# Second feed-forward product of eight layer 0 blocks in a seven-product form, and two bias additions on GpSimd

## The chip, the core and the metric

The kernel runs on one core of one Trainium2 chip, as one launch. The core has five engines that take their own instruction streams in order and signal each other by semaphores: TensorE (PE) multiplies matrices and writes to PSUM, VectorE (DVE) and ScalarE (ACT) work on tiles element by element and can read PSUM, GpSimd (POOL) does the indirect DMAs and small work, and SyncE (SP) issues most plain DMAs. The metric is the device time of the launch in microseconds (us); less is better.

## The reference

Two graph transformer layers over 2708 nodes with 512 features. What is computed in each layer, for node features h and an adjacency matrix adj:

```python
mask = adj + eye(n)
q, k, v = h @ Wq.T + bq, h @ Wk.T + bk, h @ Wv.T + bv        # 8 heads of 64
scores = einsum('nhd,mhd->hnm', q, k) / sqrt(64), -1e9 where mask == 0
ctx = softmax(scores) @ v
h1 = layer_norm(h + ctx @ Wo.T + bo, ln1_g, ln1_b)
ff = relu(h1 @ W1.T + b1) @ W2.T + b2                        # 512 -> 2048 -> 512
h2 = layer_norm(h1 + ff, ln2_g, ln2_b)
```

Everything is float32. The adjacency matrix is sparse: few nodes have more than a dozen neighbours, so the kernel attends over lists of neighbours and not over a full score matrix.

## The kernel before

The work is done by `by_edges`. The 2708 nodes are cut into 22 tiles of 128 (the last has 20), ordered by how many neighbours their nodes have, and pairs of tiles make 11 blocks. First the neighbour lists are made and layer 0's keys, values and queries are projected; then each layer runs over its 11 blocks, k = 0 to 10. Block 10 holds the short tile.

For one block, `feed_forward` is a generator with 16 steps, f = 0 to 15, one for each 128 of the 2048 hidden features. In step f, TensorE computes the hidden chunk `pf` (four products of 128x128 by 128x256, L1503, both tiles of 128 nodes at once), ScalarE writes relu of it to the tile `ft` (L1514), and TensorE does the second product of the chunk three steps back (`second(f - LAG)`, L1476): for each of the block's two tiles, 128x128 of `ft` by 128x512 of W2, added up in the PSUM tiles `a0` and `a1`. At the end the accumulators are added to the residual rows (L1547) and normed (`norm`, L1257 to L1267; its power on GpSimd, L1263).

Between the steps the main loop, written out by hand, puts other work into the same instruction streams; each engine keeps that order (the schedule is manual). In step 5 to 8 comes `keys_values` of the block before: its rows z are transposed, and the next layer's k and v are projected (L606); the key bias is added by VectorE on the way out of PSUM (L1578). In steps 10 to 12 comes `attended` for the next block: the context tile is transposed, projected to `o`, the gathered input rows are added (L1435), then the output bias in layer 0 (L1438), and the sum is normed. In step 15 `turned` transposes the normed rows into `hT` for the next block.

The attention itself is a generator too (`attend`). It is cut into chunks of up to two neighbours for each node of a tile; for a chunk, GpSimd gathers key and value rows (L1099), VectorE multiplies keys by queries (L1136) and reduces (L1142), ScalarE exponentiates (L1155) and scales values (L1162), VectorE scales the first value row (L1168) and adds up (L1175). `advance` moves it on by so many chunks in each step, from the tables PACES and PACE. Gathered rows lie in a ring of five tiles and, in layer 0 after the first queries, a sixth in the place of the query weights ("wq").

PSUM has eight banks of 512 float32 columns: two for `a0` and `a1`, three in the ring "f" for the hidden chunks, three in the ring "g" for transposes and projections.

## Time and profile before

| | us |
|---|---|
| median of three runs | 1844.04 (1843.19 to 1844.4) |
| the profiled execution, its own time | 1843.06 |
| the profiled execution, its span | 1841.3 |
| PE busy in the span | 1827.6 (99%) |
| DVE busy | 1374.8 (75%) |
| ACT busy | 947.2 (51%) |
| POOL busy | 785.4 (43%) |

The span is the stretch of the profiled execution from its first to its last instruction; its own time is a little longer, and the runs' median stands beside both. An engine's busy time is the union of its instructions. A timeline row gives start, length, engine, line, operation, tiles and how many such instructions follow each other. A window row gives, for a stretch, the busy time of PE, of its weight loads, of DVE, ACT and POOL (with counts), then the granted clock, the DMA share and GB/s. A wait row gives who waited for whom, the sum in us, how many times, and the longest. A group row ends in busy us and mean ns of one, and in the idle time before them. Layer 0's blocks run from about 250 us to 1080 us.

### The profile page before, as it was taken

To read this page: it belongs to the slowest core of one execution; us is meant where nothing else is said; L and a number is where in the kernel's file an instruction comes from. 1 tells how busy PE (TensorE), PEld (TensorE's weight loads), DVE (VectorE), ACT (ScalarE), POOL (GpSimd) and SP (SyncE) were. 2 spreads that over 40 slices of the span, in tenths; PEclk is the share of its full clock that TensorE was granted. 3 is DMA by queue.
4 is the path that set the end of the run, shared out by engine and by line. 5 is a ranking of instruction groups with operands and counts; after the bars stand their busy time and mean duration, and the time that the engine had idled before them with its cause. 6 is when DMAs were issued, how large, how long until landed. Compare 5 with 4: busy or idle time off the path is not lost.

```text
span 1841.3 us, 20983 instructions
## 1 busy us (share of the span) xinstructions
PE 1827.6 (99%) x6195; PEld 1092.1 (59%) x6195; DVE 1374.8 (75%) x2147; ACT 947.2 (51%) x3263; POOL 785.4 (43%) x745
## 2 busy tenths in 40 slices
PE   9999999999999999999999999999999999999998
PEld 4444456565666656566565544666666666666666
DVE  4996778776877767777774147977888898889853
ACT  4770445554546455555643204665655675566531
POOL 3334755543535444444431032444554554456302
PEclk9999999999999999999999999999999999999999
DMA  9997987644646455463631676835554564555300
GB/s 332 374 336 265 372 277 245 214 156 163 209 151 222 139 205 183 148 206 108 224 121 46 214 249 265 315 129 200 186 199 168 211 246 150 210 195 184 137 18 21
DMA packets 129829, 368.01 MB, mean 200 GB/s; under 512 B 14378, under 2 KB 32670, under 8 KB 129704
## 3 DMA queue, kind: packets, MB, share of 16 engines
q0 software_dynamic: 70608, 252.12, 39.3%
q1 hardware_dynamic: 48938, 92.85, 14.2%
q10 hardware_dynamic: 10158, 21.61, 3.1%
q8 instruction: 50, 0.82, 0.2%
q14 instruction: 75, 0.61, 0.1%
HBM read 315.84 MB, written 50.68 MB: 199 GB/s over the span
## 4 chain that ended last, share of the span: by engine, by line
PE 96%; DVE 2%; ACT 1%; issue 1%; DMA 0%; POOL 0%; POOLq 0%; DVEq 0%
PE pf L1503 31%; PE a L1476 30%; PE k L606 8%; PE q L606 8%; PE v L606 8%; PE o L606 8%; PE tp L1273 3%; PE a L1491 0%; DMA zT<-zT_d 0%; PE pf L1476 0%; DVE sc L1142 0%; DVE kv L1136 0%; ACT kv L1162 0%; POOL rd L1263 0%; ACT hT L1278 0%
## 5 line engine op out<-in xcount | busy, mean ns | idle before, releaser
L1503 PE MATMUL pf<-hT,w 128*128 128x256 f32 (+1 forms) x2816 | 631.4, 371 | 0.1
L1503 PEld LDWEIGHTS pf<-hT,w 128*128 128x128 f32 x2816 | 516.1, 190 | 163.0 <-issue 100.3
L1099 POOL DMA_INDIRECT kv<-kv_d,listed x420 | 506.2, 1205 | 247.7 <-issue 118.4
L1476 PE MATMUL a<-w,ft 128*128 128x512 f32 x1312 | 611.1, 592 | 0.0
L1476 PEld LDWEIGHTS a<-w,ft 128*128 128x128 f32 x1312 | 246.8, 190 | 187.4 <-issue 167.5
L1514 ACT ACTIVATE ft<-pf,b 128x256 f32<-128x256 f32 (+1 forms) x336 | 154.1, 461 | 336.3 <-PE pf L1503 328.7
L1263 POOL TENSOR_TENSOR rd<-va,mhalf 128x1 f32<-128x1 f32 (+1 forms) x88 | 81.3, 924 | 565.4 <-DVE va L1261 564.9
L1162 ACT ACTIVATE kv<-kv,p 128x64 f32<-128x64 f32 x1232 | 311.0, 335 | 5.0
L1136 DVE TENSOR_TENSOR kv<-kv,q 128x1024 f32<-128x1024 f32 (+1 forms) x222 | 257.0, 1158 | 15.9 <-DMA q<-q_d,ident_i 13.6
L1142 DVE TENSOR_REDUCE sc<-kv 128x16 f32<-128x1024 f32 (+1 forms) x222 | 258.0, 1162 | 7.6
L1175 DVE TENSOR_TENSOR acc<-acc,kv 128x1024 f32<-128x1024 f32 (+2 forms) x178 | 205.3, 1153 | 50.9 <-ACT kv L1162 34.1
L1155 ACT ACTIVATE p<-sc,listed 128x8 f32<-128x8 f32 x420 | 104.4, 299 | 144.1 <-DVE sc L1142 97.7
L606 PE MATMUL o<-wo,cT 128*128 128x512 f32 x336 | 150.9, 593 | 1.1 <-ACT cT L1278 1.1
L1168 DVE TENSOR_TENSOR kv<-kv,p 128x512 f32<-128x512 f32 (+1 forms) x178 | 122.8, 690 | 25.7 <-ACT p L1155 22.6
L1435 DVE TENSOR_TENSOR h<-o,xb 128x512 f32<-128x512 f32 (+1 forms) x44 | 30.4, 690 | 109.5 <-PE o L606 93.3
L606 PEld LDWEIGHTS o<-wo,cT 128*128 128x128 f32 x336 | 63.5, 190 | 81.0 <-issue 73.4
L731 DVE MAX8 tops<-code 128x8 f32<-128x247 f32 (+2 forms) x242 | 78.9, 400 | 27.5 <-ACT code L726 27.5
L1267 DVE SCALAR_TENSOR_TENSOR h<-h,rd,ln_b 128x512 f32<-128x512 f32 (+1 forms) x88 | 66.1, 751 | 41.1 <-POOL rd L1263 41.1
L1206 ACT ACTIVATE cx<-acc,su 128x64 f32<-128x64 f32 (+1 forms) x352 | 88.3, 333 | 12.8 <-DVE su L1198 6.2
L1162 ACT ACTIVATE acc<-kv,p 128x64 f32<-128x64 f32 (+1 forms) x352 | 88.8, 334 | 1.4
L726 ACT ACTIVATE code<-aj 128x1354 bf16<-128x1354 int32 (+1 forms) x44 | 73.6, 1724 | 25.5 <-POOL aj L720 20.6
L1278 ACT ACTIVATE cT<-tp,bv 128x128 f32<-128x128 f32 (+1 forms) x176 | 49.0, 360 | 72.9 <-PE tp L1273 72.9
(186 smaller groups left out, 1569.9 us busy)
## 6 DMA issues: line engine op xcount, KB each, us to landing
aj<-in_adj SPq DMA_DIRECT2D x42, 677.0 KB
kv_d<-kvs ACTq DMA_DIRECT2D x21, 512.0 KB
xg<-in_xT SPq DMA_DIRECT2D x19, 512.0 KB
w<-in_W SPq DMA_DIRECT2D x16, 512.0 KB
kv<-kv_d,listed POOLq DMA_INDIRECT x420
zT_d<-zT SPq DMA_DIRECT2D x22, 256.0 KB
xb_d<-h SPq DMA_DIRECT2D x21, 256.0 KB
q<-q_d SPq DMA_DIRECT2D x21, 256.0 KB
```

What stands on the lines that cost most here:

```text
L606: nc.tensor.matmul(o[:r], xs(c), wm[:, c, :], start=(c == 0), stop=(c == NC - 1))
L1099: return nc.gpsimd.indirect_dma_start(out=to, out_offset=None, in_=table[:, :], in_offset=bass.IndirectOffsetOnAxis(ap=s, axis=0), bounds_ ...
L1136: nc.vector.tensor_tensor(kv[:r, :c, :DM], kv[:r, :c, :DM], self.q[:r].unsqueeze(1).to_broadcast([r, c, DM]), ALU.mult,)
L1142: nc.vector.tensor_reduce(self.sc[:r, s0 : s0 + c, :], kv[:r, :c, :DM].rearrange("p s (h d) -> p s h d", d=DK), AX.X, ALU.add,)
L1155: nc.scalar.activation(p[:r, s, :], self.sc[:r, s, :], AF.Exp, bias=minus[:r, g, s : s + 1])
L1162: nc.scalar.activation(to[:, i, hd], kv[:r, i, DM + h * DK : DM + (h + 1) * DK], AF.Copy, scale=p[:r, s0 + i, h : h + 1],)
L1168: nc.vector.tensor_tensor(to[:, 0, :].rearrange("p (h d) -> p h d", d=DK), kv[:r, 0, DM:].rearrange("p (h d) -> p h d", d=DK), p[:r, s0, : ...
L1175: nc.vector.tensor_tensor(self.acc[:r, :c, :], self.acc[:r, :c, :], kv[:r, :c, DM:], ALU.add)
L1206: nc.scalar.activation(cx[:r, hd], self.acc[:r, 0, hd], AF.Copy, scale=self.su[:r, h : h + 1])
L1476: nc.tensor.matmul(a[:r, cols], fts[f][:, c0 : c0 + r], self.w2[f // 2][:, f % 2, cols], start=(f == 0), stop=(f == NFC - 1),)
L1503: nc.tensor.matmul(pf[:, :w], self.w1[f // 2][:, c, f % 2 * P : f % 2 * P + P], hT[:, c, :w], start=(c == 0), stop=(c == NC - 1),)
L1514: nc.scalar.activation(ft[:, :w], pf[:, :w], AF.Relu, bias=self.b1[:, f : f + 1])
```

## The change

The second product of eight blocks of layer 0 (k = 2 to 9) takes another form. Two hidden chunks f0, f1 and the two tiles of nodes make a 2x2 matrix of 128x128 blocks; the four quarters of the W2 rows of that pair make another. For the first seven of the eight chunk pairs a Strassen-Winograd form computes their product with seven block products of 256 columns (`feed_forward_by_seven`, `products`), after four VectorE additions of 128x128 (`sums`) on the hidden chunks. The products of pair j are issued two pairs behind the hidden chunks, the sums one pair behind. The results add up in four PSUM tiles, a0, a1, c0 and c1, and eight VectorE additions and one ScalarE copy put them together at the end of the block. The eighth pair is multiplied as before.

The combinations of W2's quarters that the form needs are made in block 1 by VectorE (`form`, at the steps in FORMS): one stays in place of a quarter of W2, three go to DRAM (`form_d`), and are read back pair by pair through three single tiles (`slots`) in the former place of the query weights; the sums and two more `ft` tiles lie there as well. SyncE issues those reads as each product frees its slot. In block 9 the replaced quarter is read again from W2 (`form_back`).

PSUM rings "f" and "g" have two banks instead of three in those blocks. The gathered rows of layer 0 no longer use the query weights' place. The pace of the attention in those blocks is PACE7. Two bias additions go to GpSimd: the output bias is added to the gathered input rows ahead of time (`settled_rows`, blocks 1 to 10), and the key bias of the next layer is added to the copied key rows (ScalarE copies k from PSUM) except in the last block.

```diff
+PACE7 = (0.0,) * 3 + (0.75,) * 2 + (1.2,) * 4 + (0.75,) * 2 + (0.0,) * 2 + (0.85,) * 3
+FORMED = 1
+FORMS = (3, 5, 7, 9, 13, 14, 15)
...
+    def places_of_psum(n, more=False):
+        nonlocal ps_f, ps, ps_s
+        stage.close()
+        ps_f = stage.enter_context(tc.tile_pool(name="ps_f", bufs=n, space=PSUM))
+        ps = stage.enter_context(tc.tile_pool(name="ps", bufs=n, space=PSUM))
+        if more:
+            ps_s = stage.enter_context(tc.tile_pool(name="ps_s", bufs=1, space=PSUM))
...
-        elif n < NL - 1 and all_made and not places:
-            places.extend([None] * KVB + ["wq"])
...
+        def settled_rows(self, block, xbs):
+            for g, xb in zip(block, xbs):
+                r = size(g)
+                nc.gpsimd.tensor_tensor(xb[:r], xb[:r], self.bo[:r], ALU.add)
+            self.with_bo = True
...
-                if self.n == 0:
+                if not with_bo:
                     nc.vector.tensor_tensor(h[:r], h[:r], self.bo[:r], ALU.add)
...
+        def form(self, j):
+            w, W = self.w2[j], 2 * P
+            b11, b12, b21, b22 = w[:, 0, :W], w[:, 0, W:], w[:, 1, :W], w[:, 1, W:]
+            t2, t3, t4 = self.slots
+            nc.vector.tensor_tensor(t3, b22, b12, ALU.subtract)
+            nc.vector.tensor_tensor(b12, b12, b11, ALU.subtract)
+            nc.vector.tensor_tensor(t2, b22, b12, ALU.subtract)
+            nc.vector.tensor_tensor(t4, b21, t2, ALU.subtract)
+            for i, t in enumerate((t2, t3, t4)):
+                nc.sync.dma_start(out=form_d[j, i], in_=t)
...
+            def sums(j):
+                f0, f1 = fts[2 * j], fts[2 * j + 1]
+                s = self.sums[j % 2]
+                nc.vector.tensor_tensor(s[:, 0], f1[:, P:], f0[:, P:], ALU.add)
+                nc.vector.tensor_tensor(f0[:, P:], f0[:, :P], f0[:, P:], ALU.subtract)
+                nc.vector.tensor_tensor(s[:, 1], s[:, 0], f0[:, :P], ALU.subtract)
+                nc.vector.tensor_tensor(s[:, 2], f1[:, :P], s[:, 1], ALU.subtract)
+            def products(j):
+                f0, f1, w, s = fts[2 * j], fts[2 * j + 1], self.w2[j], self.sums[j % 2]
+                t2, t3, t4 = self.slots
+                first, last = j == 0, j == J - 1
+                for to, left, right, start, stop in (
+                    (a1[:, L], f1[:, P:], t4, first, False),
+                    (c0[:, R], s[:, 1], t2, first, False),
+                    (c1[:, L], f0[:, P:], t3, first, False),
+                    (c0[:, L], f0[:, :P], w[:, 0, L], False, last),
+                    (a0[:, L], f1[:, :P], w[:, 1, L], first, False),
+                    (c1[:, R], s[:, 0], w[:, 0, R], False, last),
+                    (a0[:, R], s[:, 2], w[:, 1, R], False, False),
+                ):
+                    nc.tensor.matmul(to, left, right, start=start, stop=stop)
+                self.ask_forms(base + min(3 * j + 6, 3 * J + 3 * (k < NB - 2)))
+                if k == NB - 2:
+                    self.form_back(j)
...
+                if f % 6 < 4:
+                    ft = dn.tile([P, W], F32, tag="ft", name="ft", bufs=4)
+                else:
+                    ft = self.more_fts[f % 2]
+                nc.scalar.activation(ft, pf[:, :W], AF.Relu, bias=self.b1[:, f : f + 1])
+                fts.append(ft)
+                if f % 2 == 0 and j > 0:
+                    sums(j - 1)
+                if f % 2 and j > 1:
+                    products(j - 2)
+                yield None
+            products(J - 1)
...
+            nc.scalar.copy(u2, c0[:, L])
+            nc.vector.tensor_tensor(zA[:, L], u2, zA[:, L], ALU.add)
+            nc.vector.tensor_tensor(u2, c0[:, R], u2, ALU.add)
+            nc.vector.tensor_tensor(pair(u34), pair(c1), twice(u2), ALU.add)
+            nc.vector.tensor_tensor(zB[:, R], c1[:, R], zB[:, R], ALU.add)
+            nc.vector.tensor_tensor(zA, a0, zA, ALU.add)
+            nc.vector.tensor_tensor(zB, a1, zB, ALU.add)
+            nc.vector.tensor_tensor(zA[:, R], u34[:, R], zA[:, R], ALU.add)
+            nc.vector.tensor_tensor(pair(zB), pair(zB), twice(u34[:, L]), ALU.add)
...
-                nc.vector.tensor_tensor(kv[:r, :DM], k[:r], self.bk[:r], ALU.add)
-                plus_rest(kv[:r, :DM], k, r)
+                if block == blocks[-1]:
+                    nc.vector.tensor_tensor(kv[:r, :DM], k[:r], self.bk[:r], ALU.add)
+                    plus_rest(kv[:r, :DM], k, r)
+                else:
+                    nc.scalar.copy(kv[:, :DM], k)
...
+                if block != blocks[-1]:
+                    nc.gpsimd.tensor_tensor(kv[:, :DM], kv[:, :DM], self.bk, ALU.add)
...
+            seven = n == 0 and FORMED < k < NB - 1
+            if n == 0 and k == FORMED:
+                now.prepared()
+            if n == 0 and k in (FORMED + 1, NB - 1):
+                places_of_psum(3 - seven, seven)
...
+                if xbs and f == 9 + 2 * (k == 0):
+                    now.settled_rows(blocks[k + 1], xbs)
-                advance((PACE if k else PACES)[n][f])
+                advance((PACE7 if seven else (PACE if k else PACES)[n])[f])
...
+                if n == 0 and k == FORMED and f in FORMS:
+                    now.form(FORMS.index(f))
```

## The prediction

> **What bounds the kernel now.** First the page: busy times, the slices and the chain that ended last.
>
> ```profile
> PE 1827.6 (99%) x6195; PEld 1092.1 (59%) x6195; DVE 1374.8 (75%) x2147; ACT 947.2 (51%) x3263; POOL 785.4 (43%) x745
> PEclk9999999999999999999999999999999999999999
> PE 96%; DVE 2%; ACT 1%; issue 1%; DMA 0%; POOL 0%; POOLq 0%; DVEq 0%
> PE pf L1503 31%; PE a L1476 30%; PE k L606 8%; PE q L606 8%; PE v L606 8%; PE o L606 8%; PE tp L1273 3%; PE a L1491 0%; DMA zT<-zT_d 0%; PE pf L1476 0%; DVE sc L1142 0%; DVE kv L1136 0%; ACT kv L1162 0%; POOL rd L1263 0%; ACT hT L1278 0%
> ```
>
> TensorE is the bound, at full granted clock, and the second product (L1476) is 30% of the chain. Busy is not proof of packed, so next the timeline where a layer 0 block starts.
>
> ```profile
> 627.45 1.02 PE L1476 MATMUL a<-w,ft 128*128 128x512 f32 x2
> 628.30 7.07 PE L1503 MATMUL pf<-hT,w 128*128 128x256 f32 x32
> ...
> 656.73 1.88 PE L1476 MATMUL a<-w,ft 128*128 128x512 f32 x4
> ```
>
> 32 records in 7.07 us with the last one showing about 0.38: one record each 0.216 us. Four of 512 columns in 1.88 with a last of 0.59: 0.43 each (0.429 from start to start). L1503 has 2816 records for 22 blocks x 16 x 4 = 1408 products, so a product is two records: 0.432 us at 256 columns, 0.858 at 512. Nothing lies between them. Last, what VectorE (DVE) has left, in the window answer and in its waits of 393 to 942 us (seven blocks).
>
> ```profile
> 427.00:505.00 78.00, 78.00 (x265) 47.94 (x264) 62.18 (x85) 42.78 (x160) 36.06 (x31) 1.00 0.51 171
> 505.00:583.00 78.00, 78.00 (x264) 47.85 (x263) 58.03 (x78) 40.40 (x150) 36.82 (x33) 1.00 0.54 186
> ```
>
> ```profile
> DVE h L1435 <- PE o L606: 31.8, 11, 4.3
> DVE kvs L1578 <- PE k L606: 31.2, 13, 4.6
> DVE acc L1175 <- ACT kv L1162: 22.5, 21, 1.6
> DVE kv L1168 <- ACT p L1155: 18.1, 14, 2.0
> DVE h L1267 <- POOL rd L1263: 12.6, 28, 0.5
> ```
>
> A block lasts 78.3 us: PE all of it, DVE about 58 (third figure with a count). Its 20 idle us are 9 waiting for PE, which go when PE hurries, and 8.5 for ACT and POOL, which need not.
>
> **What the change removes.** In k=2 to 9, seven of eight chunk pairs take 7 products of 256 columns for 4 of 512: 7x0.432 = 3.02 for 3.43 us, 0.41 less. 8x7 = 56 pairs: **22.8 us**. The eighth pair costs the same (2x0.858 + 4x0.432). Each product has its own weights: PEld 190 ns fits under 216, as in L1503. A block becomes 75.5 us if PE never waits, so stalls of 2.85 us a block give everything back.
>
> **What it adds.** DVE has no 128x128 row; 128x48 takes 208 ns and 128x264 takes 421, so 128x128 is estimated at 0.29, 128x256 at 0.41. 28 operations for the sums: 8.1 us. Block end: four adds of 256 and four of 512 (0.69) for two: +3.1. L1438 and L1578 leave (2x0.69 each): -2.8. DVE goes from 58 to 66.6 of 75.5; with the 8.5 of waits that is 75.1. Full, not over. ACT gets two copies (0.57) and u2 (0.4): +1.5 on 42. POOL gets four adds of 1.27 (row below): +5.1 on 36. PSUM: rings f and g drop from three to two banks. In k=1 the forms are 28 DVE operations of 0.41 = 11.5 on 57 of 78, hidden, but those at f=13, 14, 15 each wait until the store before has left their slot; I put 1.5 us at the start of k=2 (0 to 5). Layer 0's gathered rows lose one of six places: a gather issued three chunks (13 us) ahead needs about 8, and DVE waited 0.8 us for them in all, so nothing (bound: 4 us a block if late). form_back and the bank change at k=10: nothing, no product waits for either within 5 us.
>
> Queues: SP takes its DMAs in order, and a form load waits for the product that frees its slot; behind it stand z's stores (SP idled 76 us between them) and later loads, so a late product delays only forms, and a store that waits for z at f=6 delays loads wanted 10 us on. POOL's bias adds stand behind gathers that wait for a place; the residual rows are due at 51, their adds issued near 40, so 8 us of such waiting is free, then the h add, o(1) and the chunks behind it on DVE are late.
>
> PE's clock in such a block, from its rows: products(0) at 10.4 us, z's transposes 13.4, k(0) 16.0, v(1) ends 34.5, products(2) 37.9, products(3) 44.8, o(0) ends 51.3, o(1) begins 53.5 and ends 56.9, products(5) 65.1, h's transposes 68.1, products(6) 69.0, end 75.5. Three places meet others:
>
> (a) o(1). With two g banks it takes o(0)'s bank, so DVE's h add (L1435) must be over; with three it took cx's. DVE is tied to v(1): ACT copies v (0.59), exps (0.5), eight scalings (2.0), then DVE adds 1.2 and sums 1.2: 40.0. Two attention chunks of 4.3 and sums(4): 49.8. In k=2, 4, 5 and 8 the order puts one more chunk ahead of the h add: 54.1 + 0.7 = 54.8, against 53.5: **1.3 us** late. Here the row and a rule meet:
>
> ```profile
> L944 POOL TENSOR_TENSOR kvs<-kvs,bk 128x512 f32<-128x512 f32 x20 | 25.5, 1274 | 50.3 <-ACT kvs L942 45.5 <-issue 4.8
> ```
>
> Those 20 adds ran beside MAX8, which reads one tensor and took 400 ns under them and 402 apart: by the row a POOL add costs DVE nothing. The Trainium skill (SBUF — State Buffer, "Who interferes with whom") has a DVE instruction with two SBUF inputs contend with a GpSimd one that reads SBUF, the second fully blocked. MAX8 can't show that; the chunk's multiplications and adds have two such inputs, its reduction one. Of a chunk's 4.3 us the reduction is 1.2, so an add meets a two-input operation more often than not: estimated 0.7 each, 1.8 for the two or three in this stretch. So (a) is 1.3 by the row, 3.1 by the rule, and zero if DVE runs ahead of my count; I take 2.0 x 4 = 8.0.
>
> (b) Block end. o(1)'s end + 3.6 (add, norm) + 10 to 14 (chunks, sums(6)) + 2.6 (first five end adds) gives 73 to 77 against 75.5: up to 1.7 late. Then 7.7 (rest and two norms), sums(0) 1.2, two chunk operations 2.4, ACT 2.5 + 0.5, zT 1.1: z is turned at 15.8 plus lateness, k(0) wants 16.0.
>
> (c) Forms. Their three slots are refilled between uses, normally 6 us, but products(6) follows products(5) by 3.9 us from start to start: 3.4 after the release. By the trace's completion records zT/xb stores of 256 KB landed in 2.1 to 2.7 us at 958.9 (no gathers) and the first two of four in 5.2 to 5.5 at 802.3 (with gathers). The skill's DMA: Bandwidth & Descriptors ("Anatomy of one DMA") fits 2.0 us plus bytes/436 GB/s: 2.3 for 128 KB, no stall. By the loaded row it is 1.9 or more. These loads are 384 KB a burst, not 1 MB: I take 0.7 (0 to 2.8).
>
> (b) and (c) cover each other, as waiting PE lets DVE catch up: 7.0 over all blocks. Sum: -22.8 + 8.0 + 7.0 + 1.5 = **-6.3**. The profiled execution took 1843.1 (span 1841.3 + 1.8) and gives 1836.8; the median of the runs is 1.0 above it: **1838 us**.
>
> **Rivals.** *Nearly all the gain* (0.17): DVE waits less for ACT, since it runs later than ACT here; (a) and (b) vanish: 1821 to 1830. For it: 47 us of DVE's waits are for ACT running behind PE. Against: the in-order chain through o(1). *Form loads decide* (0.13): each products(6) waits 2 to 2.8 us, 16 to 22 of 22.8 gone: 1840 to 1848. For it: loaded landings. Against: half the bytes. *DVE becomes the bound, slower* (0.30): the POOL adds hold DVE their full 5.1 us and its waits stay: 66.6 + 8.5 + 5.1 = 80.2 a block instead of 78.3, seven blocks: +13, with the start 1859. It decides once DVE loses over 3.2 us a block beyond the 75.1. For it: DVE's order is fixed and seven times a block PE now waits for it. Against: a reduction or a wait hides part of each. *The change does not do what it says*: excluded, the products are in TensorE's order.
>
> **Numbers.** Main case 0.40, 1830 to 1842. 1822 to 1860 leaves out one in ten on each side: full gain below, a DVE worse than priced above.[...] A measurement here tells 0.2% (3.7 us) from no change. Faster: 0.17 + 0.33 of the main case = 0.50; same 0.15; slower 0.30 + 0.05 = 0.35.
>
> **What would show it.** 480 fewer 512-column records (56x4 + 8x2 products) and 848 more of 256 (56x7 + 8x4), still 0.216 apart; a layer 0 block of 76 to 78 us. PE waits: (a) o on DVE's h add in k=2, 4, 5, 8; (b) k(0) on ACT zT; (c) products(6) on a form's DMA. DVE 66 to 69 a block; two-input DVE operations lengthened or delayed beside POOL adds would prove the rule. Wrong if blocks exceed 78.3 (DVE without idle), or if PE waits at products(1) to (4), where I have 6 to 10 us in hand.

## The result, and the profile after

The changed kernel takes 1874.5 us (median of 4 runs, 1870.58 to 1877.7) where the kernel before takes 1844.1 (1843.19 to 1844.4): ratio 1.0165, 95% interval 1.0143 to 1.0187. It is slower by 30 us, and the time lies outside the predicted range of 1822 to 1860. The profiled execution took 1877.7 us with a span of 1875.9.

The page's first rows, its clock row and its chain, of the changed kernel:

```profile
PE 1827.0 (97%) x6563; PEld 1169.7 (62%) x6563; DVE 1461.5 (78%) x2407; ACT 960.7 (51%) x3291; POOL 860.4 (46%) x785
PEclk9999999999999999999999999999999999999999
PE 48%; DVE 4%; ACT 2%; issue 1%; DMA 1%; POOL 0%; DVEq 0%; POOLq 0%
```

PE has 368 records more than before (6563 for 6195: 848 of 256 columns more, 480 of 512 fewer, as forecast) and is busy for 0.6 us less, although those records need 22.8 us less. These rows do not tell why: the clock row is all nines, and the shares of the chain, 96% PE before, add up to 56% here, so that it does not cover the span. The busy time of the first three changed blocks (k=2 to 4), by windows (in the order PE, PEld, DVE, ACT, POOL, with the number of instructions in brackets, then the granted clock), tells more:

```profile
392.85:481.60 88.75, 79.81 (x311) 58.53 (x310) 74.37 (x119) 41.93 (x153) 41.97 (x34) 0.96 0.63 204
481.60:567.10 85.50, 79.97 (x311) 58.06 (x310) 68.44 (x108) 41.79 (x153) 44.81 (x34) 0.96 0.60 193
567.10:644.20 77.10, 75.99 (x311) 56.61 (x311) 68.21 (x107) 43.80 (x162) 44.71 (x36) 1.00 0.69 226
```

The third block is what had been forecast: 77.1 us, PE busy 76.0. The first two take 88.8 and 85.5; PE idles 9 and 5.5 us in them, and is busy for 4 us longer with the same records, at a clock of 0.96. The seven blocks k=2 to 8 take 82.8 us on average; before, it was 78.3. VectorE is busy 66 to 74 us a block (69.4 on average), so **no engine but PE is full**: in the second block VectorE idles 17 us in all, and PE still waits 1.0 us for its h add. For whom PE waits, the waits of the whole trace say (total us, times, longest):

```profile
PE pf L1653 <- ACT ft L1664: 11.2, 7, 3.6
PE a L1643 <- DMA forms<-form_d: 9.9, 6, 2.7
PE o L620 <- DVE h L1456: 6.7, 5, 2.4
PE c L1643 <- DVE forms L1627: 4.1, 3, 2.9
PE c L1643 <- DMA forms<-form_d: 2.3, 3, 1.1
```

Four different waits: the first product (L1653) for ScalarE's Relu, the seven products (L1643) for the forms' loads, o for VectorE's h add, and the products for a VectorE sum. None of these rows is in the waits of before.

**The sum closes.** From start to start of consecutive PE records, less what a record of its size takes (0.216 us for 256 columns, 0.429 for 512, 0.109 for 128), the trace of before has 12.9 us of gaps and that of after 70.4: 16.3 ahead of the first product, 28.0 in the seven products, 12.3 ahead of or in o, the rest as before. Profiled time before, less 22.8, plus the growth of the gaps: 1843.1 - 22.8 + 57.5 = 1877.8, measured 1877.7. So the gain that was forecast is there, in full. The stalls are 57.5 us instead of the 16.5 that the prediction put against it.

**Where the seven products stand as forecast.** A product starts 0.43 us after the one before it (the timeline of PE, block k=3):

```profile
491.98 0.59 PE L1643 MATMUL a<-forms,ft 128*128 128x256 f32 x2
492.41 0.59 PE L1643 MATMUL c<-forms 128*128 128x256 f32 x2
```

**The clock.** In block k=2 the same rows look so:

```profile
404.13 0.67 PE L1643 MATMUL a<-forms,ft 128*128 128x256 f32 x2 [0.76 <-DMA forms<-form_d]
407.68 1.19 PE L1643 MATMUL c<-forms 128*128 128x256 f32 x2 [2.87 <-DVE forms L1627]
408.66 1.06 PE L1643 MATMUL c<-forms,ft 128*128 128x256 f32 x2
409.51 1.06 PE L1643 MATMUL c<-w,ft 128*128 128x256 f32 x2
```

Behind a wait of 2.87 us each product takes 0.86 instead of 0.43. The granted clock (the first figure behind POOL's) shows why:

```profile
403.24:406.66 3.42, 0.80 (x3) 0.30 (x2) 2.84 (x6) 3.42 (x15) 1.44 (x2) 1.00 0.40 132
406.66:413.48 6.82, 5.80 (x15) 4.65 (x16) 6.54 (x14) 0.24 (x1) 4.72 (x4) 0.50 0.69 212
413.48:416.90 3.42, 3.42 (x18) 2.69 (x17) 2.87 (x3) 3.03 (x12) 2.75 (x2) 1.00 0.66 201
```

The clock is halved from 406.66 us on, for 6.83 us, after a window of 3.41 us in which PE was busy for 0.80. In the whole trace 49 records lie wholly at half clock, which is 10.95 of the 57.5 us: a wait of PE can cost more than its own length. A stretch of 7 us vanishes in a row of 40 slices of 47 us.

**VectorE beside GpSimd's adds.** The timeline of VectorE, POOL and PE in block k=2:

```profile
450.59 1.22 DVE L1156 TENSOR_REDUCE sc<-kv 128x16 f32<-128x1024 f32 x1
451.73 2.78 DVE L1182 TENSOR_TENSOR kv<-kv,p 128x512 f32<-128x512 f32 x1
454.61 1.23 DVE L1189 TENSOR_TENSOR acc<-acc,kv 128x1024 f32<-128x1024 f32 x1
455.75 0.69 DVE L1456 TENSOR_TENSOR h<-o,xb 128x512 f32<-128x512 f32 x1
...
451.45 2.49 POOL L1431 TENSOR_TENSOR xb<-xb,bo 128x512 f32<-128x512 f32 x2
...
456.58 2.81 PE L620 MATMUL o<-wo,cT 128*128 128x512 f32 x6 [0.90 <-DVE h L1456]
```

The reduction, with one input, takes its 1.22 us partly under the adds. The multiplication (L1182), with two, usually takes 0.70; it starts with the adds running and ends 0.57 us after the second of them: 2.1 us lost. The h add then ends at 456.44, and o(1) has waited 0.90 us for it. Over the trace the 40 adds cost VectorE 27.1 us, 0.68 each (the forecast by the rule was 0.7): L1182 took 1917 ns on average under an add and 693 without, L1628 1844 and 293, L1156 1220 and 1220. The trace of before had one such case, which the prediction did not look at: the operation L757 with two inputs, at 142.10, runs into an add that lasts from 141.91 to 143.17 and ends 0.57 us behind it, as L1182 does here. In the kernel before, an operation of 512 columns takes 0.69.

```profile
L757 DVE TENSOR_TENSOR hot<-count,by x1: 1641/1641/1641, 142.1 to 142.1; 128x528 f32<-128x528 f32 x1
```

**Relus behind attention work.** ScalarE's timeline in block k=2, and PE's next first product:

```profile
437.42 0.45 ACT L1664 ACTIVATE ft<-pf,b 128x256 f32<-128x256 f32 x1
437.77 0.48 ACT L1169 ACTIVATE p<-sc,listed 128x8 f32<-128x8 f32 x2
438.29 2.02 ACT L1176 ACTIVATE kv<-kv,p 128x64 f32<-128x64 f32 x8
440.21 2.00 ACT L1220 ACTIVATE cx<-acc,su 128x64 f32<-128x64 f32 x8
442.12 0.48 ACT L1169 ACTIVATE p<-sc,listed 128x8 f32<-128x8 f32 x2
442.63 2.02 ACT L1176 ACTIVATE kv<-kv,p 128x64 f32<-128x64 f32 x8
444.55 0.46 ACT L1664 ACTIVATE ft<-pf,b 128x256 f32<-128x256 f32 x1
...
445.06 1.99 PE L1653 MATMUL pf<-hT,w 128*128 128x256 f32 x8 [1.97 <-ACT ft L1664]
```

ScalarE waits for nothing here. Between two Relus, in its order, stand two chunks' scalings and a division: 6.8 us. The second Relu's input was complete at about 437.9 (the two first products end there); it is read at 444.55, and only then is one of the two places f free.

Of the five longer waits of this kind (1.50 to 3.77 us) the longest, at 1017.85, is another case: there ScalarE idles, since its division waits for sums of VectorE, and two adds of GpSimd run beside these sums. Without the adds this wait is 2.06 us.

```profile
1010.46 3.52 POOL L1431 TENSOR_TENSOR xb<-xb,bo 20x512 f32<-20x512 f32 x2
...
1015.43 2.02 ACT L1220 ACTIVATE cx<-acc,su 128x64 f32<-128x64 f32 x8 [4.59 <-DVE flags L1804]
```

**Loads at products(6).** PE's and SyncE's timelines in block k=7, the last two pairs:

```profile
877.32 0.59 PE L1643 MATMUL a<-forms 128*128 128x256 f32 x2
...
877.95 1.27 SPq L1610 DMA_DIRECT2D forms<-form_d  x3
...
884.04 0.79 PE L1643 MATMUL a<-forms,ft 128*128 128x256 f32 x2 [2.66 <-DMA forms<-form_d]
```

A load is issued 0.63 us behind the start of the product that frees its slot, and is wanted 3.3 us later. In blocks k=2 to 7, where PE waited for such loads, they were there 4.4 to 6.7 us after their issue; in k=8 and 9 the 3.3 us were enough. The gaps at products(6) are 14.9 us in all, with the half clock among them.

### The profile page after: what moved, and what is told of

Its sections match the earlier page's. It is cut to its first block, busy times and chain, and to the rows that moved or that the text cites. A ratio compares the mean times of both kernels' runs of the same rounds, so it can differ in the third digit from the quotient of the medians.

```text
span 1875.9 us, 22547 instructions
## 1 busy us (share of the span) xinstructions
PE 1827.0 (97%) x6563; PEld 1169.7 (62%) x6563; DVE 1461.5 (78%) x2407; ACT 960.7 (51%) x3291; POOL 860.4 (46%) x785
## 4 chain that ended last, share of the span: by engine, by line
PE 48%; DVE 4%; ACT 2%; issue 1%; DMA 1%; POOL 0%; DVEq 0%; POOLq 0%
PE pf L1524 15%; PE a L1497 15%; PE o L620 5%; PE q L620 3%; PE pf L1653 2%; PE k L620 2%; PE v L620 2%; PE c L1643 1%; PE tp L1285 1%; PE a L1643 1%; ACT kv L1176 1%; DVE kv L1150 1%; DVE sc L1156 1%; DVE acc L1189 0%; PE a L1512 0%
## 5 line engine op out<-in xcount | busy, mean ns | idle before, releaser
L1113 POOL DMA_INDIRECT kv<-kv_d,listed x420 | 522.7, 1245 | 272.6 <-issue 93.2
L1524 PE MATMUL pf<-hT,w 128*128 128x256 f32 (+1 forms) x1792 | 393.2, 367 | 0.1
L1497 PE MATMUL a<-w,ft 128*128 128x512 f32 x800 | 373.1, 592 | 0.0
L1150 DVE TENSOR_TENSOR kv<-kv,q 128x1024 f32<-128x1024 f32 (+1 forms) x222 | 257.9, 1162 | 14.6 <-DMA q<-q_d,ident_i 12.9
L1156 DVE TENSOR_REDUCE sc<-kv 128x16 f32<-128x1024 f32 (+1 forms) x222 | 258.0, 1162 | 7.6
L1653 PE MATMUL pf<-hT,w 128*128 128x256 f32 x1024 | 236.8, 384 | 11.2 <-ACT ft L1664 11.2
L1653 PEld LDWEIGHTS pf<-hT,w 128*128 128x128 f32 x1024 | 194.6, 192 | 49.9 <-ACT ft L1664 13.4
L1497 PEld LDWEIGHTS a<-w,ft 128*128 128x128 f32 x800 | 150.1, 190 | 113.2 <-issue 101.3
L1535 ACT ACTIVATE ft<-pf,b 128x256 f32<-128x256 f32 (+1 forms) x208 | 95.0, 459 | 200.9 <-PE pf L1524 195.4
L1182 DVE TENSOR_TENSOR kv<-kv,p 128x512 f32<-128x512 f32 (+1 forms) x178 | 130.5, 733 | 27.5 <-ACT p L1169 27.4
L1664 ACT ACTIVATE ft<-pf,b 128x256 f32<-128x256 f32 x96 | 44.7, 467 | 146.9 <-PE pf L1653 146.9
L1220 ACT ACTIVATE cx<-acc,su 128x64 f32<-128x64 f32 (+1 forms) x352 | 88.2, 333 | 15.3 <-DVE flags L1804 7.5
L1176 ACT ACTIVATE acc<-kv,p 128x64 f32<-128x64 f32 (+1 forms) x352 | 88.8, 334 | 1.4
```

The source lines that it names most:

```text
L1113: return nc.gpsimd.indirect_dma_start(out=to, out_offset=None, in_=table[:, :], in_offset=bass.IndirectOffsetOnAxis(ap=s, axis=0), bounds_ ...
L1150: nc.vector.tensor_tensor(kv[:r, :c, :DM], kv[:r, :c, :DM], self.q[:r].unsqueeze(1).to_broadcast([r, c, DM]), ALU.mult,)
L1156: nc.vector.tensor_reduce(self.sc[:r, s0 : s0 + c, :], kv[:r, :c, :DM].rearrange("p s (h d) -> p s h d", d=DK), AX.X, ALU.add,)
L1176: nc.scalar.activation(to[:, i, hd], kv[:r, i, DM + h * DK : DM + (h + 1) * DK], AF.Copy, scale=p[:r, s0 + i, h : h + 1],)
L1182: nc.vector.tensor_tensor(to[:, 0, :].rearrange("p (h d) -> p h d", d=DK), kv[:r, 0, DM:].rearrange("p (h d) -> p h d", d=DK), p[:r, s0, : ...
L1497: nc.tensor.matmul(a[:r, cols], fts[f][:, c0 : c0 + r], self.w2[f // 2][:, f % 2, cols], start=(f == 0), stop=(f == NFC - 1),)
```

## The experiments

Theories, each with its place: **L**, the adds of GpSimd hold up VectorE; **R**, the forms' loads come too late for products(6); **D**, the sums fill VectorE; **B**, two PSUM places for f and g instead of three cost time by themselves; and, after the first runs, **P** and **Q**, Relus behind ScalarE's attention work with two places. In this table, "gaps" is PE's sum of gaps as above (before 12.9, after 70.4), and "by gaps" is 1843.1 - 22.8 + gaps - 12.9, to be held against the profiled run's own time. Three runs have one more wait, behind a record of 20 columns, which the sizes above leave out; it is counted in (old pace 4.5 us, the three together 3.4, three places f 1.7). Medians of the kernel before beside the runs were 1843.2 to 1843.7.

| run | median us | ratio to before, 95% interval | gaps | by gaps | profiled us |
|---|---|---|---|---|---|
| change | 1874.5 | 1.0143 to 1.0187 | 70.4 | 1877.8 | 1877.7 |
| no adds | 1859.4 | 1.0061 to 1.0103 | 48.1 | 1855.5 | 1855.9 |
| forms stay | 1856.7 | 1.0046 to 1.0080 | 47.4 | 1854.8 | 1854.7 |
| no sums | 1858.4 | 1.0044 to 1.0089 | 48.5 | 1855.9 | 1856.0 |
| old pace | 1874.8 | 1.0152 to 1.0186 | 69.7 | 1877.1 | 1877.1 |
| biases back | 1863.9 | 1.0083 to 1.0119 | 58.3 | 1865.7 | 1865.5 |
| forms last | 1860.9 | 1.0078 to 1.0131 | 49.9 | 1857.3 | 1858.4 |
| old pace, biases back, forms last | 1858.0 | 1.0070 to 1.0111 | 48.7 | 1856.1 | 1855.8 |
| three places f | 1866.7 | 1.0100 to 1.0134 | 60.1 | 1867.5 | 1867.5 |
| three places f, biases back, forms last | 1840.2 | 0.9978 to 0.9992 | 32.6 | 1840.0 | 1840.7 |
| division, biases back, forms last | 1843.7 | 0.9992 to 1.0010 | 34.6 | 1842.0 | 1841.7 |
| the same, a form earlier | 1838.4 | 0.9961 to 0.9981 | 32.4 | 1839.8 | 1839.5 |
| the same, no form operations | 1835.1 | 0.9937 to 0.9967 | 27.8 | 1835.2 | 1835.0 |

### The adds on GpSimd left out

```diff
-                nc.gpsimd.tensor_tensor(xb[:r], xb[:r], self.bo[:r], ALU.add)
+                pass
...
-                if block != blocks[-1]:
-                    nc.gpsimd.tensor_tensor(kv[:, :DM], kv[:, :DM], self.bk, ALU.add)
```

> The change with both GpSimd bias adds left out, so the key bias of the next layer and the output bias of layer 0 are missing from those blocks; all else, the seven products and their sums too, is the change (1874.5 us). Theory L (the GpSimd adds hold up VectorE, which holds up TensorE): the 25.6 us that VectorE's operations lost under the 38 adds come back, most of it on the path: 1850 to 1858. Theory R (form loads at the last pair decide) and theory D (the sums fill VectorE and its in-order queue makes ScalarE's exps and Relus late): 1868 to 1876, since neither is touched. Theory B (two PSUM places instead of three): 1868 to 1876. If waits cost double, because TensorE's granted clock falls to about 0.5 for some us after each, then a wait removed gives more than its own length, and L would show 1840 to 1850.

Measured: 1859.4, 15.1 less. L holds, 1.4 us beyond the weak end of its range. The waits of the whole trace:

```profile
PE a L1643 <- DMA forms<-form_d: 8.2, 7, 2.2
PE pf L1653 <- ACT ft L1664: 7.6, 6, 2.3
PE c L1643 <- DMA forms<-form_d: 3.5, 4, 1.8
```

o no longer waits for the h add at all; its gaps fall from 12.3 to 1.8 us. Four of the five longer waits of pf stand in this trace at the same places: those at 445.06 and 690.07 us of the change, 2.14 and 2.42 long, have here 2.14 and 2.42. Only the one at 1017.85 fell, from 3.77 to 2.06. The forms are nearly as late as they were. So L is one cause of several.

### The same adds in the kernel before

```diff
-                nc.vector.tensor_tensor(kv[:r, :DM], k[:r], self.bk[:r], ALU.add)
+                nc.scalar.copy(kv[:, :DM], k)
...
+                    nc.gpsimd.tensor_tensor(kv[:, :DM], kv[:, :DM], self.bk, ALU.add)
...
+                nc.gpsimd.tensor_tensor(xb[:r], xb[:r], self.bo[:r], ALU.add)
```

> The kernel before (1844.1 us) with the two bias adds on GpSimd as in the change, and nothing else of it. VectorE's two-input operations beside them should be as long as in the change (about 1 us more each, 0.67 us an add, 45 adds), but VectorE has 18 us idle a block here. Theory L as slack (the hold-up costs only where VectorE is full): 1843 to 1847. If the place of the hold-up is what counts (the h add is late for TensorE even here): 1850 to 1860.

Measured: 1842.3, ratio 0.9996 (0.9987 to 1.0005). The chunk's multiplication of the kernel before (L1168), minimum, median and maximum of its duration in ns, first as it is and then with the adds:

```profile
L1168 DVE TENSOR_TENSOR kv<-kv,p x67: 679/683/771, 403.9 to 983.0; 128x512 f32<-128x512 f32 x66, 20x512 f32<-20x512 f32 x1
```

```profile
L1168 DVE TENSOR_TENSOR kv<-kv,p x67: 679/682/2933, 404.7 to 985.0; 128x512 f32<-128x512 f32 x66, 20x512 f32<-20x512 f32 x1
```

One multiplication takes 2933 ns with the adds where the longest took 771 without. Over the trace the 40 adds cost VectorE 21.1 us here (27.1 in the change). The hold-up is there, and it costs no time. That VectorE's 20 idle us a block and the third place behind it take it up is the likely reason, and was not tested apart. The bias part of the change is harmless alone, and 15 us beside the other.

### The biases back on VectorE

The two adds of the first diff stand on VectorE again, with the rest of the change as it is.

> The change (1874.5 us), with both bias adds back on VectorE as in the kernel before; the seven products stay. Theory L (the adds of GpSimd cost VectorE 25.6 us, but the four adds of a block cost VectorE itself only 4x0.69 = 2.8 us, 22 in all, two of which take the place of copies by ScalarE): VectorE's work is the same within 4 us, so the gain of leaving the adds out (15 us, 1859.4) is lost for the most part: 1866 to 1874. If it is not the amount but the place of the holdups (up to 2.1 us on one operation just ahead of the h add) that TensorE waits for: 1858 to 1866.

Measured: 1863.9, 10.6 less. VectorE's own adds cost 4.5 of the 15.1 us (1863.9 - 1859.4). VectorE is busy for as long as in the change (1461.1 and 1461.5 us); what differs is that no operation just ahead of the h add is held for 2 us, and o waits for no h add any more. Place counts more than amount. Part of the gain goes to the next place: the two rows of waits for forms grow from 12.2 to 15.1 us.

### The first pair's forms kept

```diff
-            while self.asked < upto:
+            while self.asked < min(upto, 3):
```

> The change with only the first three form loads made: every pair's products take the first pair's forms, so the output is not the reference's, but no product after the first waits for a form. Time of the change: 1874.5 us. Theory R: the form waits at products(6), 9.9 us on one row and 2.3 on another, with the slow records behind them (about 0.22 us more for each record at half clock, some 16 records a wait), go: 1852 to 1860. Theory L and theory D: VectorE still sets the pace, and the room only moves the wait to the block's end: 1866 to 1874. Theory B: 1866 to 1874.

Measured: 1856.7, 17.8 less: R, too, holds, and D's view that the wait would only move does not, but for a small part: pf waits as in the change (11.3 us on its row), o's row grows from 6.7 to 9.6.

### The last pair's forms behind its other products

```diff
-                for to, left, right, start, stop in (
+                seven = [
...
+                if last:
+                    seven = seven[3:] + [
+                        (*seven[0][:4], False), (*seven[1][:4], True), (*seven[2][:4], True)
+                    ]
...
+                for to, left, right, start, stop in seven:
```

> The change (1874.5 us), with the last pair's seven products in another order: the four that need no form first, the three with a form behind them, so that the time from a slot's release to its next use grows by 4x0.432 = 1.7 us to about 5.1. Theory R: the landings have a median of about 3 us and reach 6, the waits at products(6) were 1.5 to 2.8 us, so most of them go: of the 17.8 us that the kept forms gave, 10 to 16 come back, 1858 to 1865. If the loads are late because they start late (behind other work of their queue), not because they are short of 2 us: under 5 us, 1870 to 1875.

Measured: 1860.9, 13.6 less, of the 17.8 that there are. From issue to use there are now 5.0 us instead of 3.3 (1.73 more), which is nearly enough for the 4.4 to 6.7 above: 2.2 us of waits for forms are left. The page's median over the block is shorter,

```profile
forms<-form_d SPq DMA_DIRECT2D x168, 128.0 KB, 3.6
```

but it rests on the 21 landings that the trace tells, from all places of a block.

### No sums

The 28 VectorE operations a block are left out, and the products take the hidden chunks themselves in place of the sums.

> The change without the 28 VectorE operations a block that form the sums of the hidden chunks; the seven products take the chunks themselves, so the second product is wrong, but TensorE has the same number of records with the same forms and the same loads. Time of the change: 1874.5 us. Theory D: VectorE has 8 us a block less, its exps' scores come on time, ScalarE's Relus too: waits for pf, o and the sums go, 1833 to 1842. Theory L: the adds still hold VectorE, but with 8 us of slack a block they are hidden: also 1833 to 1845, so this run tells D and L apart only with the run without the adds. Theory R: the form loads are as late as before, 1852 to 1868. Theory B: two PSUM places make pf and o wait all the same, 1855 to 1870.

Measured: 1858.4, far from the 1833 to 1845 of D and L. With 8 us of VectorE work less a block, and VectorE idle for more, pf still waits 11.0 us for ScalarE, the forms still come late (8.4 us on two rows) and o still waits for the h add (3.9 us). D falls as the one cause: VectorE's amount of work is not what PE waits for. L's view that 8 us of slack would hide the adds falls too.

### Two places alone

```diff
+            if n == 0 and k in (2, NB - 1):
+                places_of_psum(2 if k == 2 else 3)
```

> The kernel before (1844.1 us) with the two PSUM rings of the first product and of the projections at two places instead of three during blocks 2 to 9 of layer 0, and nothing else. Theory B (the places are what makes TensorE wait): 1852 to 1870, with waits of pf for ScalarE and of o for VectorE's h add. Theories L, R and D: VectorE and ScalarE are on time in the kernel before, so 1844 to 1849.

Measured: 1845.6, ratio 1.0005 (0.9996 to 1.0014). B by itself falls: in the kernel before, one wait of pf of 0.9 us comes in.

### The chunks by the old list

```diff
-                advance((PACE7 if seven else (PACE if k else PACES)[n])[f])
+                advance(((PACE if k else PACES)[n])[f])
```

> The change (1874.5 us), with the attention chunks spread over the seven-product blocks by the list of the kernel before (PACE) instead of PACE7: the same work, another order of ScalarE's and VectorE's queues. In the trace of the change TensorE waited for a first-product place five times by 1.50 to 3.77 us, and the same five waits, to 0.01 us in part, stand in the traces without the adds, without the sums and with the forms kept. Theory P (the chunk order puts up to 7.7 us of ScalarE work ahead of a Relu that one of only two places waits for; the old list has 7.2 us or more ahead of one twice, the new one four times): two or three of the five waits go, with the slow records behind them, 1864 to 1870. If they come from TensorE being faster than ScalarE whatever the order: 1872 to 1877.

Measured: 1874.8, no change, where P had 1864 to 1870. The waits did move: those at 524, 690 and 849 us went. But three new ones of 2.02 us came early in a block (490, 575 and 731 us), where six first products stand in a row, others of 2.41 and 4.12 us (768 and 934 us), and the one at 1018 us grew from 3.77 to 4.49, so that the row of pf's waits grew from 11.2 to 17.8 us. Wherever the chunk and its division are put, they stand ahead of some Relu.

### Old pace, biases back and forms last together

> The change with the three edits together: chunks by the old list, biases on VectorE, the last pair's forms last; it computes all that the reference does. If the causes add up: 1874.5 less what each gives alone, estimated 6 + 6 + 13, so 1846 to 1852. If one place covers another (a TensorE that waits at one place waits less at the next): 1853 to 1862. If all that is left is the shorter product: below the kernel before, 1835 to 1843.

Measured: 1858.0. Biases and forms add up to 24 us, and 16.5 come: pf has gaps of 19.8 us (16.3 in the change), the longest of 4.3 at 920 us and 3.4 at 1001. The old list is no mend.

### Three places f

```diff
-            c0, c1 = (ps_s.tile([P, DM], F32, tag=f"c{i}", name=f"c{i}") for i in range(2))
+            c0 = ps_s.tile([P, DM], F32, tag="c0", name="c0")
+            c1 = c0
...
-        ps_f = stage.enter_context(tc.tile_pool(name="ps_f", bufs=n, space=PSUM))
+        ps_f = stage.enter_context(tc.tile_pool(name="ps_f", bufs=3, space=PSUM))
```

> The change (1874.5 us) with the two accumulators c0 and c1 laid together in one PSUM place, so that their sums run into each other and the output is not the reference's, and the place that comes free given to the ring of the first product: three places f instead of two. The number and order of all instructions is that of the change. Theory Q (a Relu that stands behind 4.3 to 7.7 us of ScalarE's in-order attention work holds one of only two places): the waits of pf for ScalarE, 11.2 us on the row of waits and 16.3 us with slow records, go: 1858 to 1864. Rival S (ScalarE is late as a whole, whatever the places): the wait moves to the products, that need the same Relu one pair later: 1870 to 1875.

Measured: 1866.7, between the two. Two rows of the waits of its whole trace:

```profile
PE o L620 <- DVE h L1456: 11.3, 5, 4.5
...
PE pf L1654 <- ACT ft L1665: 1.5, 1, 1.5
```

The waits of pf go, as Q says, from 11.2 to 1.5 us: two places beside that order of ScalarE's work are their cause. But o's wait for the h add grows from 6.7 to 11.3, and its wait for ScalarE's transposed context (cT) from 1.1 to 5.2: PE comes earlier to a VectorE that is held by the adds, and to a ScalarE that is as late as before. The rival had the wait move to the products; it moved to o (gaps of 22.0 us instead of 12.3).

### All three causes mended

The edits of three of the runs above (three places f, biases back, forms last) in one kernel. With c0 and c1 in one place it does not compute the layer; it prices the waits.

> The change with all three causes mended at once: c0 and c1 laid together and three places f (the output is not the reference's), biases back on VectorE, the last pair's forms last. If the causes add up: 1874.5 less 10.6 (biases), 13.6 (forms last) and what three places give alone (estimated 13): 1834 to 1842, below the kernel before. If VectorE with the biases is then the next to bind: 1845 to 1855. TensorE's waits left: the first pair of block 2, 3 to 5 us, since VectorE is behind after the 28 operations that made the forms.

Measured: 1840.2, ratio 0.9985 (0.9978 to 0.9992). Apart, the three give 7.8, 10.6 and 13.6 us, 32.0 in all; together 34.3. In this combination they add up.

### The division on VectorE

```diff
+            if by_vector:
+                nc.vector.tensor_tensor(
+                    cx[:r].rearrange("p (h d) -> p h d", d=DK),
+                    self.acc[:r, 0, :].rearrange("p (h d) -> p h d", d=DK),
+                    self.su[:r].unsqueeze(2).to_broadcast([r, NH, DK]),
+                    ALU.mult,
+                )
+                return cx
```

This stands in for eight ScalarE operations in blocks 2 to 9 (L1220), with biases on VectorE and forms last.

> The change with biases on VectorE and the last pair's forms last, and the division of the attention sums, eight ScalarE operations of 2.0 us for a tile, made by one VectorE operation of about 0.7 us in blocks 2 to 9; it computes all that the reference does. Theory Q: the bunches ahead of a Relu fall from 7.7 to 5.3 us and from 4.3 to 2.4, so the waits of pf (1.5 to 3.8 us) shrink by 1.9 each and mostly go: 1838 to 1846. Theory D: VectorE, 1.4 us a block fuller, becomes late instead, o and the sums wait: 1850 to 1858.

Measured: 1843.7, ratio 1.0001 (0.9992 to 1.0010). With 5.4 us of ScalarE's work ahead of the Relus that had 7.9, pf waits 4.8 us in all, in spite of two places. Theory D's price for the fuller VectorE does not show.

### The forms' making

Open was the wait at the first pair of block 2, 2.9 us on its row, with 2.6 us lost to half clock behind it. Four runs on the base of the last one. The first leaves out the operations that make the forms:

```diff
-            nc.vector.tensor_tensor(t3, b22, b12, ALU.subtract)
-            nc.vector.tensor_tensor(b12, b12, b11, ALU.subtract)
-            nc.vector.tensor_tensor(t2, b22, b12, ALU.subtract)
-            nc.vector.tensor_tensor(t4, b21, t2, ALU.subtract)
-            for i, t in enumerate((t2, t3, t4)):
+            for i, t in enumerate((b21, b22, b12)):
```

> The same base (1843.65 us) without the 28 VectorE operations that make the forms in block 1: the stores take raw quarters of the matrix, so the second product is wrong; loads, stores and products are as many as before. It prices the forms. The forecast put 1.5 us (0 to 5) at the start of block 2 for them. Theory E: the wait of 3.05 us and what follows it go, and block 1 is not touched: 1838 to 1841. Theory F: 1842 to 1845.

The second makes one form earlier:

```diff
-FORMS = (3, 5, 7, 9, 13, 14, 15)
+FORMS = (3, 5, 7, 9, 11, 13, 15)
```

> The kernel with biases on VectorE, the last pair's forms last and the division on VectorE (1843.65 us), with one edit: in block 1 the form of pair 4 is made at f=11 instead of f=13, and that of pair 5 at 13 instead of 14. In every kernel with sums TensorE waited 2.6 to 3.1 us at the first pair of block 2 for a sum of VectorE. Theory E (VectorE is behind from the forms made at f=13, 14 and 15, which stand between it and that sum): one form, 1.6 us of VectorE, moves away from the end: the wait shrinks by 1 to 2 us: 1841 to 1843. Theory F (the wait is VectorE's attention work of the block's start, whatever the forms): 1843 to 1845.

The third changes the order of the first pair's products, and the fourth has both edits:

```diff
+                if first:
+                    seven = [seven[i] for i in (3, 4, 0, 2, 5, 1, 6)]
+                    for i, start in enumerate((True, True, True, True, False, False, False)):
+                        seven[i] = (*seven[i][:3], start, False)
```

> The same base (1843.65 us), with one edit: in the first pair of each block the four products that need no sum come first, then the three that need one, so that the first sum is wanted 3x0.432 = 1.3 us later than at present, where it is wanted by the second product. By theory E as by theory F the wait at the first pair of block 2 shrinks by 1.3 us, and may lose the slow records behind it (1.0 to 2.4 us): 1840 to 1843. If a late sum only moves the wait to the next pair: 1843 to 1845.

> The same base (1843.65 us) with the earlier form and the late sums together; it computes all that the reference does. Theory E: 1838 to 1842, faster than the kernel before (1843.2) by 0.1 to 0.3%. Theory F: 1841 to 1844, the same as before.

Measured: without the form operations 1835.1 (8.5 us less); with one form earlier 1838.4, ratio 0.9971 (0.9961 to 0.9981), **faster than the kernel before** by 0.3%; with the late sums 1845.6 (1.0001 to 1.0019), and with both 1841.4 (0.9981 to 0.9999). E holds, and gave more than it was expected to: the forms are the cause. Of the 5.2 us that one earlier form gives by the medians, the two traces show 2.2; the runs of the base spread over 8 us. VectorE's timeline of the change at the end of block 1 shows how:

```profile
393.28 0.43 DVE L1595 TENSOR_TENSOR forms<-w,forms 128x256 f32<-128x256 f32 x1 [1.23 <-DMA form_d<-forms]
...
399.19 0.42 DVE L1595 TENSOR_TENSOR forms<-w,forms 128x256 f32<-128x256 f32 x1
399.54 0.68 DVE L1568 TENSOR_TENSOR h<-a,h 128x512 f32<-128x512 f32 x1
...
406.76 0.28 DVE L1625 TENSOR_TENSOR forms<-ft 128x128 f32<-128x128 f32 x1
```

A form waits 1.23 us until the store before it has left its slot; behind the last form stand the block's end and two norms, 7.2 us, and behind these the first sum, which PE wants at 404.6. With one form moved ahead, PE waits 1.65 us there instead of 2.88, and no half clock follows. With late sums and with both edits the range had been 1840 to 1843 and 1838 to 1842: the first missed. My edit with late sums rested on a wrong count: of the four products put first, one takes the difference that VectorE leaves in the chunk's own place (L1626), so it waits for VectorE too, and another waited 1.71 us for its form. Why that kernel came out 1.9 us above its base is not settled; its o had gaps of 8.5 us, against 4.1.

## Why the prediction was wrong

The gain was right. The step that failed is the sum of the stalls, 16.5 us in the prediction and 57.5 measured: the term (c) was too small, the places f had no term, (a) and the forms' making were too small, and half clock had no term.

- **The gain of 22.8 us** was right: records, spacing, and the sum by gaps, which meets all twelve edited kernels of the table within 1.2 us.
- **VectorE's amount** was right: 0.29 us for a 128x128 operation (0.28 to 0.31 measured), 66.6 us a block (69.4 measured on average, 3.2 of them under the adds). The step built on it was not. "Full, not over" was to decide between gain and loss, and so was the rival of a VectorE that binds by its amount; yet VectorE idled in blocks where PE waited for it, and taking 8 us of work from each block did not bring the gain back. What binds is the moment at which one operation in a fixed order is reached.
- **(a), 8.0 us, o behind the h add:** right in the kind of wait, and the rule of the Trainium skill (SBUF — State Buffer, "Who interferes with whom") about two-input operations beside GpSimd was right against the row that seemed to say otherwise; L757 in the trace of before spoke for it. The part by the row (1.3 us a block from one more chunk) was not there: with the adds gone or on VectorE, o waited for no h add. The blocks were not those forecast either: k=2, 4, 5 and 8 were charged with 2.0 us each, and o's gaps were 1.1, 0, 0.4 and 4.3 us there, and 1.3, 0.9 and 2.6 in k=3, 6 and 7. By size it failed: o's gaps were 12.3 us, and without the adds 15.1 us came back. The hold-ups came two at a time (2.1 us on one operation) and half clock followed some.
- **(c), 0.7 us of each block's (b) and (c), form loads at products(6):** the term that was mis-sized most. The loaded row gave 1.9 us or more, and a rival had it at 2 to 2.8 with 16 to 22 us in all; I took 0.7 since half the bytes would land sooner. Half the bytes did not: they took 4.4 to 6.7 us where PE waited, against 5.2 to 5.5 in the loaded row, and keeping the forms gave 17.8. The estimate of 2.3 us from the Trainium skill (DMA: Bandwidth & Descriptors, "Anatomy of one DMA") did not hold for these loads of SyncE beside gathers; the section gives its fit for DMAs of GpSimd's path. The window from issue to use was 3.3 us, not 3.4. Of (b) there was next to nothing: k's row of waits for zT is 0.6 us in the whole trace.
- **Places f, priced at nothing** ("rings f and g drop from three to two banks" with only g's consequence followed): the step that is missing. PE's times in a block were laid out for VectorE's chain, not for ScalarE's order, where up to 7.9 us of work stand between two Relus. It cost 16.3 us of gaps, a few of them through the adds (at 1017.85), and 7.8 when mended alone. Two places alone cost nothing in the kernel before (1.0005), so no wait there pointed at them.
- **The forms' making, 1.5 us (0 to 5):** 8.5 on the mended base, above its range. The block's end and the norms behind the last form (7.2 us) were not counted.
- **Waits taken at their own length:** 10.95 us of the gaps are half clock.
- **The side:** the rival on the slow side had 0.30 and 1859; the measured time is 15 us above that, from four small causes at once, where each rival had one. That three of them add up (34.3 together, 32.0 apart) is what the prediction's "waiting PE lets DVE catch up" had excluded.

## What to carry to other kernels

An engine at 99% with every other below 80% is not sure to take a shorter product as gain: list, for each place where it meets another engine's in-order queue, what stands ahead of the operation that it waits for and how many buffers lie between, and do so for every ring that loses a place. A hold-up was free while it had slack (the adds in the kernel before, two places in the kernel before) and had a price (15.1 and 7.8 us) beside others that used the same slack. Price a transfer by the loaded row, and put a short reuse distance last in its group.

## What the runs showed of the hardware

**Half clock after waits of 2 us.** In the traces of the change and of fourteen kernels made from it, I took the waits of PE (gaps of 0.4 us or more in the stretch from 385 to 1100 us) with no other within 7 us. Many of them are the same wait in several kernels.

| wait, us | number | followed by half clock |
|---|---|---|
| 0.40 to 2.02 | 115 | 0 |
| 2.03 to 2.6 | 30 | 13 |
| 2.6 to 3.2 | 10 | 4 |
| over 3.2 | 10 | 9 |

By the clock records, half clock began between 1.3 us before the restart and 1.4 behind it, lasted 3.41 or 6.83 us, and cost 1.0 to 2.7 us.

What decides is not the wait's length alone. In each of the 18 traces the changes between full and half clock lie whole multiples of 3.413 us apart. Cut into windows on that grid, the same stretch has 3600 windows at full clock and 54 at half:

| window at | PE busy in it | number | next window at half clock |
|---|---|---|---|
| full clock | under 0.41 | 33 | 33 |
| full clock | 0.41 to 0.46 | 16 | 10 |
| full clock | over 0.46 | 3551 | 0 |
| half clock | up to 0.80 | 11 | 11 |
| half clock | over 0.82 | 43 | 0 |

So a wait has to leave a window of this grid busy for less than about 0.41 to 0.46, which is 1.8 to 2.0 us of idling. A wait of 2.05 us does so when it falls inside one window; one of 3.38 us (three edits with the old pace, at 1001 us), split over two windows that were busy for 0.60 and 0.47, did not.

The Trainium skill (TensorE: Matmul & The Clock Gate, "Part 1: The HAM clock gate") has the clock fall after an idle window of about 3.4 us, whose phase runs free, and return after about 3.4 busy. The window's length, its grid and the return agree with that; that it has to be idle throughout does not: windows with PE busy for up to 0.46 were enough.

**What a GpSimd add costs VectorE depends on what it meets.** An add of 1.27 us cost nothing during a reduction (1220 ns with and without) and up to its whole length during a two-input operation; two in a row held one operation of 0.70 us for 2.78.
